# A gated delta rule and a ternary layer on one core: where the chain of states starts, how the first inverses are grouped, and the order of the last units

## The chip, the cores and the metric

The kernel runs on one core of one Trainium2 chip. The metric is the time of one execution on the device in microseconds; the profile gives the span of one profiled execution, from its first to its last instruction.

## The reference, cut to what matters

The input x has 4 sequences of 4096 tokens of 512 numbers; there are 16 heads of 32. All is fp32.

```python
def _L0_attn_ref(x, Wv, Wo, Wg, Wb):          # x is layer-normalised already
    rk = x.reshape(Bb, Tt, H, dd)
    rk = rk / max(norm(rk, axis=-1), 1e-12)   # keys
    wk = rk shifted by one token              # write keys
    v = (x @ Wv.T).reshape(Bb, Tt, H, dd)
    gate = sigmoid(x @ Wg.T)
    beta = sigmoid(x @ Wb.T)
    def step(S, inp):
        pred = einsum('bhk,bhkd->bhd', wk_t, S)
        err = (v_t - pred) * b_t[..., None]
        S = S + wk_t[..., None] * err[..., None, :]
        o = einsum('bhk,bhkd->bhd', rk_t, S) * g_t[..., None]
        return (S, o)
    ...
    return out @ Wo.T
def _L0_ffn_ref(x, weight, ln_gamma, ln_beta):
    xn = layernorm(x) * ln_gamma + ln_beta
    beta = mean(abs(weight))
    w_q = clip(round(weight / (beta + EPS)), -1, 1)
    gamma = max(abs(xn))                       # over the whole tensor
    xq = clip(xn * QB / gamma, -QB + EPS, QB - EPS)
    return (xq @ w_q) * (gamma * beta / QB)
x = x + layernorm(attn(layernorm(x)))
x = x + layernorm(ffn(layernorm(x)))
```

The state S of a head is carried through all 4096 tokens, so the recurrence is serial. The number gamma is a maximum over all tokens, so it is known only behind the last one.

## The kernel before, in words

**Units.** A unit is 32 tokens of each of the 4 sequences, which fills 128 partitions; there are NU = 128 units. Within a unit the recurrence is solved in blocks: a 32 x 32 triangular matrix per head and sequence is built from the products of the keys, inverted, and applied to values and keys; only the state is then carried from unit to unit.

**Blocks of unit k** (they need no state). `load` (L149), `x_stats` (L155, VectorE), `x_norm` (L158, GpSimd), `keys` (L167: ACT makes the tile h, which is stored to DRAM at L171), `keys_turn` (L173: TensorE transposes, ACT copies hT and hN, GpSimd puts a column of the next unit into hN at L189), `key_squares`, `key_sums` (L204), `key_norms` (GpSimd, the power at L213), `values` and `values_rest` (TensorE L233 and L265), `values_out` (VectorE L253), `writes` (the mask times beta, L280), `gates`, `grams` (TensorE L298), `blocks` (ACT L309), `masked` (L317; stored to DRAM). The two mask products run on VectorE for the units of the first group and on GpSimd for all others (`masks`, L270).

**Inverses.** Units are taken in groups, `sizes = [4, 4, 6, 6]` and then 8 each, the last group being 4. `gather` (L325) brings the group's matrices from DRAM so that one partition holds whole matrices, and `invert` (L334) inverts them on VectorE in place: for s from 1 to 30 one product (L343) and one add (L349), each depending on the one before. A group of any size has 60 such instructions; their length grows with the size. The work of a group is spread evenly over a span of steps, between the step in which its units' blocks are there and the step three before its first unit is due in the chain.

**Chain of unit i.** `fetch`, `fetch_inverse`, `expand` (ACT L408), `apply` (TensorE L420), `errors` (TensorE L437 and L444; VectorE makes e at L450 and o at L455), `outputs` (GpSimd L459), `grow` (TensorE L470; VectorE adds into the state, four instructions of L476). Then, one to five units later: `out_turn`, `project` (TensorE L511), `residual` (VectorE L520), `x1_stats`, `x1_norm`, `x1_turn`, `largest` (VectorE L559 fills gmax), `ternary` (TensorE L570) and `finish` (VectorE L582, four stores at L586). `x1_stats`, `project` and `ternary` each use ACT for a sum of squares (L497) and GpSimd for its power (L94).

**Order.** The order of work on every engine is written out by hand. A step is either a plan step (unit i of the chain and unit k of the blocks, list `plan`, L667) or a lead step (blocks of unit k alone, list `lead`, L682). There are `START = sizes[0] + 6` = 10 lead steps, 0 to 9; then plan steps for i = -3, -2, -1 (the chain is only prepared); then from i = 0 every plan step is followed by a lead step until the blocks are 21 units ahead. So the chain's unit 0 is in step 13, eight pairs (a plan step and a lead step) follow, then plain plan steps; behind the blocks' last unit the plan steps hold chain work only. Numbers such as 0.3 in the lists are the places where a share of the inverse work is put. `in_order` (L724) ties each engine to the order in which the instructions are written. All stores and loads are issued by SP, in that same order. One-time work on the weights stands in front and, as `between` (L756), behind the steps 0, 1 and 2.

**Behind the chain.** gamma is made by a maximum on VectorE and a reduction over the partitions on GpSimd (`partition_all_reduce`, L795). The layer's output was computed without the clip; a list of the units whose largest xn reaches the clip is then made (L805 to L834: `ps_gm`, `place`, `hit`, `todo`), and a loop (L840) computes these units anew from xn and x1 in DRAM. With these inputs it runs for one unit.

Of the kernel before, what the change touches and what calls it, by code (L numbers as in the profile page):

```python
# [8 lines left out]
F32 = mybir.dt.float32  # L9
# [4 lines left out]
P = 128  # L14
# [8 lines left out]
def kernel(  # L23
# [85 lines left out]
    with ExitStack() as ph1:  # L109
# [27 lines left out]
        sizes = [4, 4, 6, 6]  # L137
# [29 lines left out]
        def keys(i):  # L167
            my = cx[i]
            my["h"] = wk.tile([P, D], F32, tag="h", name=f"h_{i}")
            nc.scalar.activation(my["h"], my.pop("x"), AF.Identity, bias=my["nb"], scale=my["rs"])  # L170
            nc.sync.dma_start(out=h_d[i], in_=my["h"])  # L171
# [98 lines left out]
        def masks(i):  # L270
            return nc.vector if i < sizes[0] else nc.gpsimd
# [307 lines left out]
        def finish(i):  # L579
# [4 lines left out]
            )  # L584
            for b in range(B):
                nc.sync.dma_start(out=out[b, i * DH : (i + 1) * DH, :], in_=y[quarters(b), :])  # L586
# [50 lines left out]
        def ternary_scale():  # L637
            nc.vector.tensor_reduce(part, wq, AX.X, ALU.add, apply_absolute_value=True)
            nc.vector.tensor_reduce(bsum, part, AX.X, ALU.add)
            ones = wk.tile([P, D], F32, tag="junk", name="ones", bufs=1)  # L640
            nc.gpsimd.memset(ones[:, :P], 1.0 / (D * D))
# [40 lines left out]
        lead = (  # L682
# [6 lines left out]


        FAR = 4 * NP + 5
        START = sizes[0] + 6
# [3 lines left out]
        for i in range(-3, NU + 6):  # L696
            k += 1
            steps.append((i, k))
            if i >= 0 and k < i + FAR:
                k += 1  # L700
                steps.append((None, k))
# [41 lines left out]
        for f in (x_stats, x_norm, keys, keys_turn, key_squares):  # L743
            do(f, 0)
        for f in (x_stats, x_norm, keys):
            do(f, 1)
        do(load, 4)
        do(key_sums, 0), do(key_norms, 0)
        turn_weight("wv", wvbT)
        do(keys_turn, 1), do(key_squares, 1)  # L750
        turn_small("wb", wvbT[:, :, D : D + H])
        turn_small("wg", wvbT[:, :, D + H :])
        do(x_stats, 2), do(x_norm, 2)
        for t_ in tbds:
            nc.vector.memset(t_, 0.0)
        between = {  # L756
            0: (ternary_scale,), 1: (lambda: turn_weight("wo", woT, wm), ternary_round),
            2: (lambda: centred(woT, wm), ternary_centre),
# [3 lines left out]
        for n, (i, k) in enumerate(steps):  # L762
# [5 lines left out]
            for item in lead if i is None else plan:  # L768
# [12 lines left out]

        for n in range(2):
# [4 lines left out]
    with ExitStack() as ph2:  # L787
        once = ph2.enter_context(tc.tile_pool(name="once2", bufs=1))
        wk = ph2.enter_context(tc.tile_pool(name="wk2", bufs=1))
        TOP = QB - EPS  # L790

        gpart = once.tile([P, 1], F32, name="gpart")
        nc.vector.tensor_reduce(gpart, gmax, AX.X, ALU.max)
        gamma = once.tile([P, 1], F32, name="gamma")
        nc.gpsimd.partition_all_reduce(gamma, gpart, P, bass_isa.ReduceOp.max)  # L795
        qs = once.tile([P, 1], F32, name="qs")
        nc.vector.reciprocal(qs, gamma)
        nc.vector.tensor_scalar_mul(qs, qs, QB)
        ys = once.tile([P, 1], F32, name="ys")
        nc.vector.tensor_scalar(ys, gamma, beta, 1.0 / QB, ALU.mult, ALU.mult)  # L800
        ys2 = once.tile([P, 1], F32, name="ys2")
        nc.vector.tensor_tensor(ys2, ys, ys, ALU.mult)


        num = once.tile([P, NU], mybir.dt.int32, name="num")  # L805
        nc.gpsimd.iota(num, pattern=[[1, NU]], base=0, channel_multiplier=0)
        col = once.tile([P, NU], F32, name="col")
        nc.vector.tensor_copy(col, num)
        nc.gpsimd.iota(num[:, 0:1], pattern=[[1, 1]], base=0, channel_multiplier=1)
        row = once.tile([P, 1], F32, name="row")  # L810
        nc.vector.tensor_copy(row, num[:, 0:1])
        ahead = once.tile([P, NU], F32, name="ahead")
        nc.vector.tensor_scalar(ahead, col, row, None, ALU.is_gt)
        ps = bank("ps_gm")
        nc.tensor.transpose(ps[:, :P], gmax, ident)
        umax = once.tile([P, 1], F32, name="umax")
        nc.vector.tensor_reduce(umax, ps[:, :P], AX.X, ALU.max)
        again_ = once.tile([P, 1], F32, name="again")
        nc.vector.tensor_scalar(again_, umax, qs, TOP, ALU.mult, ALU.is_le)
        nc.vector.tensor_scalar(again_, again_, -1.0, 1.0, ALU.mult, ALU.add)  # L820
        ps = bank("ps_place")
        nc.tensor.matmul(ps[:, 0:1], lhsT=ahead, rhs=again_, start=True, stop=True)
        place = once.tile([P, 1], F32, name="place")
        nc.vector.tensor_copy(place, ps[:, 0:1])
        hit = once.tile([P, NU + 1], F32, name="hit")
        nc.vector.tensor_scalar(hit[:, :NU], col, place, again_, ALU.is_equal, ALU.mult)
        both = once.tile([P, 2], F32, name="both")
        nc.vector.tensor_copy(both[:, 0:1], row)
        nc.vector.memset(both[:, 1:2], 1.0)
        ps = bank("ps_list")  # L830
        nc.tensor.matmul(ps[0:1, :NU], lhsT=both[:, 0:1], rhs=hit[:, :NU], start=True, stop=True)
        nc.tensor.matmul(ps[0:1, NU : NU + 1], lhsT=both[:, 1:2], rhs=again_, start=True, stop=True)
# [61 lines left out]
```

## Time and profile before

| | us |
|---|---|
| median of 3 runs | 2456.01 (2452.75 to 2457.76) |
| the profiled execution | 2456.91 |
| its span | 2454.2 |
| TensorE busy | 2336.5 |
| VectorE busy | 1907.9 |
| ScalarE (ACT) busy | 1680.2 |
| GpSimd (POOL) busy | 1684.3 |

How to read the profile's rows: a digit string shows the busy share of each fortieth of the span (61 us), in tenths. A row of a timeline gives start and length in us, engine, line, operation, output and inputs, and, in brackets, for how long the engine was idle before and what ended it. PE is TensorE, PEld its weight loads, DVE is VectorE, SPq the queue of SP. In a table of stretches each engine has its busy time and its number of instructions, then the clock that TensorE was granted, the busy share of the DMA engines and what they moved. In the chain that ended last, "issue" is time in which the engine waited for nothing that the profile shows.

### The profile page before, as it was taken

The numbers are of one execution on the slowest core, as the hardware profiler recorded it, in microseconds if no ns is written. First come the engines' busy times: TensorE is split into PE (matmuls) and PEld (weight loads), VectorE is DVE, ScalarE is ACT, GpSimd is POOL, SyncE is SP. The second block draws the span as 40 slices with busy tenths as digits, with TensorE's granted clock in tenths as the row PEclk, the third lists the DMA queues.
The fourth block names the chain that finished last, engine by engine and source line by source line (L and its number), as shares of the span: only waits on it lengthen the run. The fifth ranks groups of instructions, "written<-read, shape, count | busy, mean of one in ns | idle before, by whom it ended". The sixth has DMA issues, their size and how long they took to land.

```text
span 2454.2 us, 69871 instructions
## 1 busy us (share of the span) xinstructions
PE 2336.5 (95%) x26657; PEld 1554.0 (63%) x26657; DVE 1907.9 (78%) x2928; ACT 1680.2 (68%) x3484; POOL 1684.3 (69%) x2702
## 2 busy tenths in 40 slices
PE   5778999999999999999999999999999999999995
PEld 4556666666666666666666666666666666555552
DVE  5888777988788888888788887878888787887642
ACT  5556667776777777677777767777776777665652
POOL 5988877877777776767777677777767776422221
PEclk8889999999999999999999999999999999999997
DMA  5576666767676766676676767667676766746442
GB/s 152 142 188 167 196 172 191 197 198 200 203 202 192 205 183 202 178 208 183 193 198 177 215 179 206 184 195 195 173 218 177 208 184 184 191 140 169 141 120 64
DMA packets 765372, 445.93 MB, mean 182 GB/s; under 512 B 591056, under 2 KB 591056, under 8 KB 765040
## 3 DMA queue, kind: packets, MB, share of 16 engines
q1 hardware_dynamic: 765040, 441.48, 64.4%
q8 instruction: 212, 3.47, 0.6%
q14 instruction: 120, 0.98, 0.1%
HBM read 205.07 MB, written 235.14 MB: 179 GB/s over the span
## 4 chain that ended last, share of the span: by engine, by line
PE 83%; POOL 6%; DVE 4%; ACT 2%; issue 2%; DMA 1%; SPq 1%; DVEq 0%; POOLq 0%; ACTq 0%
PE ps_wo L511 19%; PE ps_y L570 16%; PE ps_v L233 9%; PE ps_v L265 7%; PE ps_ds L470 6%; PE ps_u L420 5%; PE ps_gram L298 5%; PE ps_f L444 5%; PE ps_w L420 4%; PE ps_f L437 3%; PE ps_oT L491 2%; POOL rn L213 2%; PE ps_xn L491 2%; PE ps_hT L179 2%; DVE na L349 1%
## 5 line engine op out<-in xcount | busy, mean ns | idle before, releaser
L511 PE MATMUL ps_wo<-woT,oT 128*128 128x512 f32 x1024 | 473.7, 605 | 1.6 <-ACT oT L504 1.6
L570 PE MATMUL ps_y<-wq,xn 128*128 128x512 f32 x1024 | 462.2, 594 | 0.0
L343 DVE TENSOR_TENSOR pr<-na 128x336 f32<-128x336 f32 (+25 forms) x540 | 437.1, 809 | 12.4 <-DMA x<-in_L_attn_x_dram 0.6
L349 DVE TENSOR_TENSOR na<-na,pr 128x336 f32<-128x336 f32 (+25 forms) x540 | 431.5, 799 | 12.2
L213 POOL TENSOR_TENSOR rn<-ss,mhalf 128x16 f32<-128x16 f32 x128 | 379.3, 2964 | 10.7
L476 DVE TENSOR_TENSOR state<-ps_ds,state 32x512 f32<-32x512 f32 x508 | 347.9, 685 | 20.3 <-PE ps_ds L470 14.9
L309 ACT COPY nat<-ps_gram 32x512 f32<-32x512 f32 x512 | 294.7, 576 | 33.8 <-PE ps_gram L298 29.4
L408 ACT COPY tbd<-q 32x512 f32<-32x512 f32 x512 | 313.1, 612 | 7.0
L532 POOL TENSOR_SCALAR vpe_c<-acc_c 128x1 f32<-128x1 f32 x128 | 24.3, 190 | 422.5 <-ACT junk_c L497 422.5
L511 PEld LDWEIGHTS ps_wo<-woT,oT 128*128 128x128 f32 x1024 | 184.0, 189 | 200.9 <-issue 183.7
L233 PE MATMUL ps_v<-wvbT,hN 128*128 128x288 f32 x1024 | 281.6, 419 | 26.6 <-POOL hN L189 26.6
L570 PEld LDWEIGHTS ps_y<-wq,xn 128*128 128x128 f32 x1024 | 185.2, 191 | 185.2 <-issue 184.5
L552 ACT ACTIVATE xn<-ps_xn,lnb,lng 128x128 f32<-128x128 f32 x512 | 192.2, 457 | 100.2 <-PE ps_xn L491 100.2
L253 DVE TENSOR_TENSOR v<-ps_v,nrm 128x256 f32<-128x256 f32 x256 | 107.3, 420 | 182.2 <-issue 140.9
L497 ACT ACTIVATE junk_y<-ps_y 128x512 f32<-128x512 f32 x128 | 76.5, 597 | 250.1 <-PE ps_y L570 250.1
L265 PE MATMUL ps_v<-wvbT,hN 128*128 128x256 f32 x1024 | 247.3, 385 | 0.3 <-DVE v L253 0.3
L233 PEld LDWEIGHTS ps_v<-wvbT,hN 128*128 128x128 f32 x1024 | 189.5, 195 | 73.6 <-POOL hN L189 29.3
L420 PE MATMUL ps_u<-tbd,v 128*32 128x128 f32 x4096 | 209.0, 276 | 0.0
L420 PE MATMUL ps_w<-tbd,h 128*32 128x128 f32 x4096 | 205.7, 273 | 0.1
L265 PEld LDWEIGHTS ps_v<-wvbT,hN 128*128 128x128 f32 x1024 | 188.2, 194 | 22.4 <-issue 1.0
L520 DVE SCALAR_TENSOR_TENSOR x<-ps_wo,rstd_b,xr 128x512 f32<-128x512 f32 x128 | 96.1, 751 | 113.5 <-POOL rstd_b L94 100.7
L450 DVE TENSOR_TENSOR e<-ps_f,bet 128x512 f32<-128x512 f32 x127 | 87.7, 690 | 116.8 <-PE ps_f L444 116.8
(146 smaller groups left out, 4373.7 us busy)
## 6 DMA issues: line engine op xcount, KB each, us to landing
x<-in_L_attn_x_dram SPq DMA_DIRECT2D x512, 64.0 KB
h_d<-h SPq DMA_DIRECT2D x128, 256.0 KB
v_d<-v SPq DMA_DIRECT2D x128, 256.0 KB
nat_d<-nat SPq DMA_DIRECT2D x128, 256.0 KB
na<-nat_d SPq DMA_DIRECT2D x256, 128.0 KB
q_d<-na SPq DMA_DIRECT2D x64, 512.0 KB
q<-q_d SPq DMA_DIRECT2D x256, 128.0 KB
h<-h_d SPq DMA_DIRECT2D x128, 256.0 KB
```

The costliest lines, as they stand in the source:

```text
L213: nc.gpsimd.tensor_tensor(rn, ss, mhalf, ALU.pow)
L233: nc.tensor.matmul(ps[:, : half + 2 * H], lhsT=my["hN"][:, k, :], rhs=wvbT[:, k, half:], start=(k == 0), stop=(k == KC - 1),)
L265: nc.tensor.matmul(ps[:, :half], lhsT=my["hN"][:, k, :], rhs=wvbT[:, k, :half], start=(k == 0), stop=(k == KC - 1),)
L309: nc.scalar.copy(nat[s].rearrange("p (j q) t -> p j q t", j=HQ), ps[s].rearrange("p j (q t) -> p j q t", q=NQ)[:, :, :, s],)
L343: nc.vector.tensor_tensor(prs[s], bcast(na[:, :, s, s + 1 :], [P, np_, s, m], 2), bcast(na[:, :, :s, s], [P, np_, s, m], 3), ALU.mult,)
L349: nc.vector.tensor_tensor(na[:, :, :s, s + 1 :], na[:, :, :s, s + 1 :], prs.pop(s), ALU.add)
L408: nc.scalar.copy(tbds[i % NBD][s, :, s], q[s])
L420: nc.tensor.matmul(ps[quarters(j), qq * P : (qq + 1) * P], lhsT=src[:, hd * DH : (hd + 1) * DH], rhs=tbd[:, j * NQ + qq, :], start=True, s ...
L476: nc.vector.tensor_tensor(S[s, :, :, s], psd[s].rearrange("p b (q d) -> p b q d", q=NQ)[:, :, :, s], S[s, :, :, s], ALU.add,)
L511: nc.tensor.matmul(ps, lhsT=oT[:, k, :], rhs=woT[:, k, :], start=(k == 0), stop=(k == KC - 1))
L552: nc.scalar.activation(xn[:, k * P : (k + 1) * P], ps[:, k * P : (k + 1) * P], AF.Identity, bias=lnb[:, k : k + 1], scale=lng[:, k : k + 1],)
L570: nc.tensor.matmul(ps, lhsT=xn[:, k * P : (k + 1) * P], rhs=wq[:, k, :], start=(k == 0), stop=(k == KC - 1),)
```

## The change

- The groups of inverses are 2, 2, 2, 2, 4, 4 units, then 8 each (the last one has 8, too). `START` is 6: six lead steps, then i = -3, -2, -1, then unit 0 of the chain in step 9. Pairs go on until the blocks are 21 units ahead again, so there are twelve of them. Groups 0 to 6 have the steps 4-5, 6-7, 8-10, 11-14, 15-18, 19-26 and 27-33 (before, groups 0 to 4 had 6-9, 10-14, 16-22, 23-31 and 32-37).
- The lead steps in front have a list of their own, in which loads, statistics, keys and squares are one unit further ahead and the turn of the keys comes early; the lead steps of the pairs keep the old list, now named `beside`. The order in front is changed to fit, and the weight work is spread behind the steps 0 to 3.
- The stores of h for units 0, 1 and 2 are issued by ACT's queue; so are the output stores of units 125 to 127 and half of the output stores of the loop.
- Plan steps end with i = 126. The rest of the last units is written out in an order of its own. In it, the reduction of gamma over the partitions is made by TensorE transposes and VectorE, and the list of units is made before `ternary(127)` and the last three `finish`.
- The tiles behind the chain are cut from the pools in use; no new pool is opened.

```diff
-        sizes = [4, 4, 6, 6]
+        sizes = [2, 2, 2, 2, 4, 4]
...
-            nc.sync.dma_start(out=h_d[i], in_=my["h"])
+            (nc.scalar if i < 3 else nc.sync).dma_start(out=h_d[i], in_=my["h"])
...
-            return nc.vector if i < sizes[0] else nc.gpsimd
+            return nc.vector if i < 4 else nc.gpsimd
...
+            queue = nc.scalar if i > NU - 4 else nc.sync
             for b in range(B):
-                nc.sync.dma_start(out=out[b, i * DH : (i + 1) * DH, :], in_=y[quarters(b), :])
+                queue.dma_start(out=out[b, i * DH : (i + 1) * DH, :], in_=y[quarters(b), :])
...
-        lead = (
+        beside = (
...
+        lead = (
+            (AHEAD, 6, load), (AHEAD, 4, x_stats), (AHEAD, 4, x_norm), (AHEAD, 2, keys_turn),
+            (AHEAD, 1, key_sums), (AHEAD, 1, key_norms), (AHEAD, -1, blocks), (AHEAD, 0, values),
+            (AHEAD, 2, key_squares), (AHEAD, 3, keys), (AHEAD, -1, masked), 0.3,
+            (AHEAD, 0, values_out, half), (AHEAD, 0, values_rest), (AHEAD, 0, writes), 0.35,
+            (AHEAD, 0, values_out, 0), (AHEAD, -1, gates), (AHEAD, 0, grams), 0.35,
+        )
...
-        START = sizes[0] + 6
+        START = 6
...
-        for i in range(-3, NU + 6):
+        for i in range(-3, NU - 1):
...
-        for f in (x_stats, x_norm, keys, keys_turn, key_squares):
-            do(f, 0)
-        for f in (x_stats, x_norm, keys):
-            do(f, 1)
-        do(load, 4)
-        do(key_sums, 0), do(key_norms, 0)
+        for f, i in (
+            (x_stats, 0), (x_norm, 0), (keys, 0), (keys_turn, 0), (load, 4),
+            (x_stats, 1), (x_norm, 1), (keys, 1), (load, 5), (key_squares, 0),
+            (x_stats, 2), (x_norm, 2), (key_sums, 0), (key_norms, 0), (keys_turn, 1),
+        ):
+            do(f, i)
...
-            0: (ternary_scale,), 1: (lambda: turn_weight("wo", woT, wm), ternary_round),
-            2: (lambda: centred(woT, wm), ternary_centre),
+            0: (ternary_sums,), 1: (ternary_scale, lambda: turn_weight("wo", woT, wm)),
+            2: (ternary_round, lambda: centred(woT, wm)), 3: (ternary_centre,),
...
-            for item in lead if i is None else plan:
+            for item in plan if i is not None else lead if n < START else beside:
...
+        N = NU - 1
+        for f, i in (
+            (again, N), (errors, N), (out_turn, N - 1), (x1_turn, N - 3), (outputs, N),
+            (x1_stats, N - 2), (finish, N - 5), (x1_norm, N - 2), (largest, N - 3),
+            (project, N - 1), (out_turn, N), (x1_turn, N - 2), (project, N), (residual, N - 1),
+            (x1_stats, N - 1), (x1_norm, N - 1), (largest, N - 2), (residual, N),
+            (ternary, N - 4), (finish, N - 4), (x1_stats, N), (x1_norm, N), (x1_turn, N - 1),
+            (ternary, N - 3), (largest, N - 1), (x1_turn, N), (largest, N), (finish, N - 3),
+            (ternary, N - 2),
+        ):
+            do(f, i)
...
-        nc.gpsimd.partition_all_reduce(gamma, gpart, P, bass_isa.ReduceOp.max)
...
+        nc.vector.tensor_reduce(umax, ps[:, :P], AX.X, ALU.max)
+        nc.tensor.transpose(ps[0:1, P : 2 * P], umax, ident)
+        gamma, gall = some(1), some(P)
+        nc.vector.tensor_reduce(gall[0:1, 0:1], ps[0:1, P : 2 * P], AX.X, ALU.max)
+        nc.vector.tensor_copy(gall[0:1, 1:], gall[0:1, 0:1].to_broadcast([1, P - 1]))
+        nc.tensor.transpose(ps[:, 2 * P : 2 * P + 1], gall[0:1, :], ident[0:1, 0:1])
+        nc.vector.tensor_copy(gamma, ps[:, 2 * P : 2 * P + 1])
...
+        do(ternary, N - 1)
...
+        do(ternary, N)
+        for i in range(N - 2, NU):
+            do(finish, i)
...
-                nc.sync.dma_start(out=out[b, bass.ds(u * DH, DH), :], in_=y[quarters(b), :])
+                (nc.sync if b % 2 == 0 else nc.scalar).dma_start(
+                    out=out[b, bass.ds(u * DH, DH), :], in_=y[quarters(b), :]
+                )
```

## The prediction

> **What bounds the kernel now.** The page comes first, for the share of each engine over the span.
>
> ```profile
> PE   5778999999999999999999999999999999999995
> DVE  5888777988788888888788887878888787887642
> POOL 5988877877777776767777677777767776422221
> PEclk8889999999999999999999999999999999999997
> ```
>
> TensorE is full except in the first four slices and the last one. Between them nothing that the change touches can gain. So the question has two parts: the head (up to about 420 us) and the tail (from the last unit of the chain). In the timeline of VectorE every unit of the chain is marked by its one `e` (L450). I write e(i) for its start: e(0) at 150.18, e(8) at 344.23, e(12) at 420.65, e(126) at 2378.38 us. From e(12) to e(105) they lie 17.89 us apart. Second view: busy time in stretches cut at these marks.
>
> ```profile
> core 0: us, PE busy (x) PEld busy (x) DVE busy (x) ACT busy (x) POOL busy (x), PEclk, DMA share, GB/s
> 86.30:97.90 11.60, 9.39 (x64) 7.36 (x63) 11.22 (x20) 5.45 (x12) 10.80 (x15) 0.83 0.66 172
> 150.18:173.29 23.11, 17.14 (x242) 13.24 (x241) 20.76 (x43) 14.92 (x27) 17.98 (x29) 0.98 0.62 164
> 218.67:244.94 26.27, 22.17 (x252) 15.75 (x252) 21.98 (x34) 17.76 (x36) 21.50 (x34) 0.94 0.65 172
> 244.94:268.65 23.71, 23.17 (x258) 16.11 (x259) 19.73 (x40) 15.29 (x32) 21.61 (x35) 1.00 0.68 206
> 383.42:401.31 17.89, 17.89 (x209) 11.97 (x210) 12.65 (x25) 13.02 (x28) 11.87 (x21) 1.00 0.53 171
> 2250.00:2300.00 50.00, 47.14 (x612) 28.57 (x611) 35.30 (x57) 29.74 (x66) 13.97 (x29) 1.00 0.53 148
> ```
>
> The first row is a lead step (blocks only): VectorE is busy 97% of it and GpSimd 93%; TensorE, though listed as busy, runs at a clock of 0.83. The next three are pairs (a chain step and a lead step), at 23 to 26 us; then a plain step. The last row holds 3.7 chain-only steps of 13.53 us, so a chain unit is 12.75 us of TensorE. A block unit is then 17.89 - 12.75 = 5.1, and a pair needs 23.0 of TensorE.
>
> Third, the timeline of VectorE and GpSimd in a lead step, for the price of the inverses.
>
> ```profile
> 84.14 1.68 DVE L343 TENSOR_TENSOR pr<-na 128x396 f32<-128x396 f32 x1
> 85.86 0.57 DVE L349 TENSOR_TENSOR na<-na,pr 128x396 f32<-128x396 f32 x1
> 84.13 1.26 POOL L317 TENSOR_TENSOR nat<-nat,mb 128x512 f32<-128x512 f32 x1
> 122.64 0.22 DVE L343 TENSOR_TENSOR pr<-na 128x60 f32<-128x60 f32 x1
> 145.46 0.66 DVE L343 TENSOR_TENSOR pr<-na 128x480 f32<-128x480 f32 x1
> ```
>
> Start to start, 60 elements take 0.26 us and 480 take 0.70: 0.197 us fixed and 1.05 ns an element. Every group, whatever its size, is 60 such instructions in one dependent row, with 9,920 elements for each pair of units: 11.8 + 10.4 us for 2 units = 22.2; 4 units 32.6, 6 units 43.0, 8 units 53.4.
>
> Fourth, the chain that ended last, in the tail.
>
> ```profile
> 2417.54 0.30 DVE gpart L793
> 2417.84 3.95 issue
> 2421.78 0.38 POOL gamma L795
> 2422.23 6.62 issue
> 2429.11 0.60 POOL rstd_y L94
> ```
>
> From 2417.8 to 2429.1 everything stands behind one GpSimd reduction, listed as 0.38 us, with 4.0 us before it and 6.6 behind it in which GpSimd shows no work.
>
> **The head, part by part.** *First keys stored by ACT's queue.* Now the store of h(0) is issued by SP at 14.39, though h(0) is ready at 7.7, because SP first has loads of x and of three weights in its row. The tile of h(2) is that of h(0), so its write waits:
>
> ```profile
> 21.68 0.81 ACT L170 ACTIVATE h<-x,nb_a,rstd_a 128x512 f32<-128x512 f32 x1 [4.76 <-DMA x<-in_L_attn_x_dram]
> ```
>
> The Trainium skill speaks against this edit (DMA: Bandwidth & Descriptors, "Issuing engines are not separate DMA queues": queues of different engines share the same 16 DMA engines, so only issue time is saved). By the rule the store would still share the DMA with 2 MB of weights and the gain would be near zero; by the row it is issue order that counts, 14.39 against about 7.8, and up to 4.8 us are free. What follows limits it: the first ps_v runs from 17.89 to 21.4, so the first v comes at 21.8 instead of 24.17. I take 2.4 us, with 0 and 2.4 as bounds. ACT pays 3 issues of about 0.4 us (the SP rows' price), in time in which it waits.
>
> *Steps 0 to 3.* From v(0) to v(4) VectorE now needs 42.4 us (24.17 to 66.58). Of these, ACT waits 4.5 for ps_beta and 4.6 for wm, and GpSimd waits 20.3 us in six places for mv_a. The new lead order (statistics and keys one unit earlier, the turn of keys first, the weight work over four steps) can remove the two ACT waits and some of the rest: I take 31 us, 7.8 a step, near the 7.2 to 7.7 between GpSimd's rn (L213) at steps 4 and 5 now, where no weight work stands. Bounds 27 and 42. The first inverse then starts at 21.8 + 31 + 1 = 54 (48 to 66) instead of 75.4.
>
> *Steps 4 to 8: groups of 2 units.* Group 0 has steps 4 and 5, group 1 steps 6 and 7, group 2 steps 8 to 10. VectorE also does 2.1 us of block work a step (from starts: st 0.72, aggr 0.10, ss 0.59, v twice 0.34). Sum: 22.2 + 22.2 + 7.4 + 5 x 2.1 + 0.6 (the last mask) = 62.9 us. Now a lead step's share is 32.6/4 + 2.1 = 10.2 and steps take 10.2 to 11; then it is 13.2, so VectorE alone sets the pace. Add the fight for the port: the first row of the third view took 1.68 where its neighbour of the same size took 0.57, while GpSimd's mask ran. The Trainium skill (SBUF — State Buffer, "SBUF: two separate sides") says that a VectorE instruction with two SBUF inputs and a GpSimd one that reads SBUF exclude each other for the whole instruction. By the rule each of the two masks of a step would cost up to 1.1 to 1.3 us, 13 us in five steps; group 0 now shows seven hits in four steps, 7.4 us in all. I take 7 (0 to 13), and 2 for small waits. e(0) = 54 + 62.9 + 7 + 2 = 126 (111 to 140), 24 us earlier than now, where four steps at the present pace (44 us) would have been expected.
>
> *Twelve pairs instead of eight.* VectorE's fixed part of a pair is 2 x 2.1 + 5.9 (state 2.79, y, x1, gmax, e, o about 0.63 each) = 10.1. With the groups' shares: pair 0: 24.9; 1 and 2: 21.2; 3 and 4 (4 units in 4 steps): 26.4; 5 to 8: 18.2; 9 to 11 (8 units in 7 steps): 25.4. The larger of this and TensorE's 23.0, added up, is 24.9 + 46 + 52.8 + 92 + 76.2 = 291.9. The same sum for the present eight is 23.1 + 161 = 184.1, measured 194.05, so 1.24 more for each. For twelve: 291.9 + 14.9 = 307 (292 without it; 320 if the dense six take 29 as the pair at 218.67 would with 4.4 us more VectorE work). e(12) = 126 + 307 = 433. At e(12) both kernels have the same 33 block steps behind them, and the same plan ahead. Now it is at 420.65, and this already holds the step from pairs to plain ones (21.3 instead of 17.9); the changed kernel still has that ahead: +3.4. Head: 433 + 3.4 - 420.65 = +15.8 us (between -15 and +35).
>
> **The chain-only stretch.** VectorE then does 5.9 + 53.4/8 = 12.6 a step while a group of 8 runs. Now that is so from e(107) to e(113), and these steps take 14.05 on average; with the last group of only 4 they take 13.53. The changed kernel's last group has 8, over ten such steps: 4 more x 0.52 = +2. The rest of the plan is unchanged.
>
> **The tail.** Order of TensorE behind the last ps_f (2391.8): oT and xn, wo(126) until 2396.6, oT(127), wo(127) until 2401.2 (now 2405.7, since y(123) goes ahead of it), y(123), xn(126), y(124), xn(127), y(125). From wo(127) to gmax(127) the rows give about 11.5 us, with two waits on ACT: gmax is complete at 2412.7 (now 2417.5), y(125) ends then, too. Now comes the replacement of the reduction: three transposes and their copies at 0.75 + 0.2 us a hop (the hop of ps_place and place now: 2431.28 to 2432.03), gamma at 2415.7, qs and again_ at 2416.5; y(126) sits ahead of ps_place and ends at 2419; place, hit and list as now give todo at 2421.3 instead of 2434.1. So 11.3 us of stall become 3 of hops and 2.5 of y(126). Then some is given back: the stores of y(125) wait on ACT behind the squares of y(127) (2425.3); y(127) takes the same tile, so waits until they land (about 2429), and ys, ys2 and the loop's first xq stand behind it on VectorE: xq at 2430.1 instead of 2439.15. From there to the end the rows give 15.05; one unit in the loop, its 6.3 us of ps_again at a clock of 0.62[...], and 1 us less as two queues store. End 2444: -10.5 (-15 to -6; lower if ps_again keeps its clock, 2.9 us).
>
> The remaining edits (masks by number, ones by VectorE, iota earlier, tiles from the old pool) cost below 1 us each beside waits of several us, and nothing is late behind them.
>
> **Sum.** 15.8 + 2 - 10.5 = +7 us by the middle values; the largest part, the twelve pairs, I set 2 us lower (305), since light pairs may take up what dense ones leave. So +5 against a profiled execution of 2456.9 (span 2454.2 and 2.7 around it). The median shown is 2456.0: 2461.
>
> **Rivals.** *Main case, 0.48:* as summed, own range 2453 to 2470. VectorE's saturation in steps 4 to 8 and in six pairs returns what the early chain brings; the tail pays most of it back. *The early chain holds, 0.27:* lead steps keep 10.7 us, pairs keep 24.3: e(0) at 108 to 116, e(12) at 400 to 408, head -10 to -15, with the tail 2431 to 2440. For it: VectorE is busy only 80% from 80 to 400 us, and pairs at 280 to 300 us have holes. Against: 13.2 us of instructions don't fit in 10.7. This is the case on the other side; it decides when the dense pairs stay below 25.5 us and e(0) comes before 117. *GpSimd as bound, 0.20:* at 21.5 busy and 34 gaps of 0.08 a pair, it is 92% full already, and a denser VectorE stretches it (10.8 us a lead step against 7.2 without inverses): dense pairs at 30, 2472 to 2482. *The lead order doesn't help, 0.05:* steps 0 to 3 keep 42 us, so e(0) at 137: 2472.
>
> **The numbers.** About 0.2% (4.9 us) is what a measurement of this kernel tells from no change: bounds 2451.1 and 2460.9. Of the main case I put 0.22 within, 0.23 above and 0.03 below. The early-chain case is faster by 0.25 and 0.02 within; the two others are slower. Faster 0.28, same 0.24, slower 0.48. The range from 2435 to 2478 leaves out the outer part of both rivals.
>
> **What would show it.** e(0) near 126; lead steps 4 to 7 at 13 to 14 us with VectorE at 95%; pairs 3, 4, 9, 10 and 11 at 27 to 28, the others below 25; e(12) at 428 to 438; ten chain-only steps near 14.05; the hole on TensorE behind gmax gone, todo near 2421 plus the shift of the head. It is wrong if dense pairs take 24 us, or if the first inverse starts before 48 us.

## The result, and the profile after

The changed kernel takes 2482.7 us (median of 4 runs, 2478.91 to 2483.43) against 2456.84 beside it: a ratio of 1.0105 (95% interval 1.0088 to 1.0123). It is slower by 26 us where +5 was forecast, and lies outside the range. Its profiled span is 2481.3 us against 2454.2: +27.1.

The page of the changed kernel, busy shares of the slices (62 us each here):

```profile
PE   6578998999999999999999999999999999999997
...
DVE  4889868887878788887888888888888888788442
...
POOL 5568878777777777777777777777677777522221
PEclk8789999999999999999999999999999999999998
```

TensorE now has 6 5 7 8 in the first four slices, where it had 5 7 7 8, and an 8 in the seventh where it had a 9. The place of the loss is read from the marks e(i), the starts of VectorE's `e`:

| mark | before | after | after minus before |
|---|---|---|---|
| first instruction of an inverse | 75.41 | 70.86 | -4.6 |
| e(0) | 150.18 | 136.81 | -13.4 |
| e(9) | 365.54 | 366.14 | +0.6 |
| e(12) | 420.65 | 452.16 | +31.5 |
| e(18) to e(106) | | | +34.1 |
| e(126) | 2378.38 | 2414.63 | +36.25 |
| end of the span | 2454.2 | 2481.3 | +27.1 |

The chain does start 13 us earlier. It loses 45 us in the twelve pairs, keeps the lag for 90 steps, and gets 9 us back in the tail. Stretches of the changed kernel, with the columns of the same view before:

```profile
core 0: us, PE busy (x) PEld busy (x) DVE busy (x) ACT busy (x) POOL busy (x), PEclk, DMA share, GB/s
80.00:100.00 20.00, 10.48 (x59) 7.73 (x60) 18.83 (x45) 7.90 (x14) 11.82 (x18) 0.76 0.40 92
207.95:236.30 28.35, 23.61 (x257) 16.27 (x255) 27.00 (x51) 18.39 (x38) 22.98 (x35) 0.90 0.81 185
335.03:366.14 31.11, 26.70 (x261) 17.72 (x261) 17.99 (x37) 17.62 (x37) 20.64 (x38) 0.89 0.57 158
366.14:395.62 29.48, 26.23 (x272) 18.02 (x272) 25.88 (x41) 19.05 (x40) 24.08 (x33) 1.00 0.79 187
543.30:561.19 17.89, 17.89 (x209) 11.97 (x209) 13.71 (x20) 13.01 (x28) 14.21 (x25) 1.00 0.77 180
2290.00:2340.00 50.00, 46.69 (x562) 28.03 (x555) 25.86 (x42) 31.38 (x67) 12.69 (x30) 1.00 0.68 176
```

First a stretch of lead steps: VectorE is 94% busy, as forecast, and TensorE's clock is down to 0.76. Then three pairs. The one at 207.95 has VectorE at 95%. The one at 335.03 takes 31.1 us although *no* engine is near full: VectorE 18.0, GpSimd 20.6, TensorE 26.7 at a clock of 0.89. The forecast put this pair at 23.0 plus 1.24. The last two rows, a plain step and the chain-only stretch, have the old pace.

In front, ScalarE (ACT) waited twice for the weight work before the change (timeline of ACT; the brackets give the idle time before):

```profile
29.49 0.16 ACT L644 COPY beta<-ps_beta 128x1 f32<-128x1 f32 x1 [4.46 <-PE ps_beta L643]
...
48.84 2.56 ACT L630 ACTIVATE woT<-woT,wm 128x512 f32<-128x512 f32 x4 [4.59 <-DVE wm L628]
```

It still does so twice in the changed kernel, and it still stands once, for 5.89 us, in the first 25 us (4.76 before, in a row that the prediction shows):

```profile
22.87 0.35 ACTq L172 DMA_DIRECT2D h_d<-h  x1
23.27 0.58 ACT L184 COPY hT<-ps_hT 128x512 f32<-128x512 f32 x1 [5.89 <-DMA x<-in_L_attn_x_dram]
...
52.29 2.56 ACT L632 ACTIVATE woT<-woT,wm 128x512 f32<-128x512 f32 x4 [5.25 <-DVE wm L630]
...
64.49 2.56 ACT L632 ACTIVATE wq<-wq,part 128x512 f32<-128x512 f32 x4 [5.04 <-DVE part L630]
```

The copy hT reads no x. The row above it, of ACT's own queue, shows whose wait it is: the third store of h, ready since 17.4, is issued only at 22.87, once an earlier load of x has landed that shares its semaphore, and the copy stands behind it.

And the tail, where the reduction of gamma stood (timeline of VectorE):

```profile
2450.16 0.29 DVE L832 TENSOR_REDUCE many<-ps_gm 128x1 f32<-128x128 f32 x1
...
2451.65 0.16 DVE L838 COPY many<-ps_gm 128x1 f32<-128x1 f32 x1 [0.31 <-PE ps_gm L837]
...
2455.39 0.16 DVE L848 COPY many<-ps_place 128x1 f32<-128x1 f32 x1 [2.76 <-PE ps_place L847]
...
2456.43 0.28 DVE L854 CAST todo<-ps_list 1x129 int32<-1x129 f32 x1 [0.50 <-PE ps_list L852]
```

The maximum over the partitions is there 1.65 us after the first reduction starts; the list of units (`todo`) is complete at 2456.7. Less the lag of 36.25 at e(126) that is 2420.5; 2421.3 was forecast.

### The profile page after: what moved, and what is told of

It is laid out like the page before. It is cut to its first block, busy times and chain, and to the rows that moved or that the text cites. A ratio compares the mean times of both kernels' runs of the same rounds, so it can differ in the third digit from the quotient of the medians.

```text
span 2481.3 us, 70012 instructions
## 1 busy us (share of the span) xinstructions
PE 2350.8 (95%) x26659; PEld 1563.0 (63%) x26659; DVE 1934.2 (78%) x3053; ACT 1680.3 (68%) x3485; POOL 1676.9 (68%) x2700
## 4 chain that ended last, share of the span: by engine, by line
PE 78%; DVE 9%; POOL 3%; DMA 3%; SPq 3%; issue 2%; ACT 1%; ACTq 0%; DVEq 0%; POOLq 0%
PE ps_wo L512 18%; PE ps_y L571 15%; PE ps_v L234 8%; PE ps_v L266 7%; PE ps_ds L471 5%; PE ps_u L421 4%; PE ps_gram L299 4%; PE ps_f L445 4%; PE ps_w L421 4%; DVE pr L344 3%; DVE na L350 3%; PE ps_f L438 3%; PE ps_oT L492 2%; PE ps_xn L492 2%; PE ps_hT L180 2%
## 5 line engine op out<-in xcount | busy, mean ns | idle before, releaser
L344 DVE TENSOR_TENSOR pr<-na 128x120 f32<-128x120 f32 (+8 forms) x600 | 450.1, 750 | 14.0 <-issue 0.3
L350 DVE TENSOR_TENSOR na<-na,pr 128x120 f32<-128x120 f32 (+8 forms) x600 | 444.3, 740 | 14.4
L214 POOL TENSOR_TENSOR rn<-ss,mhalf 128x16 f32<-128x16 f32 x128 | 377.9, 2953 | 10.6
L310 ACT COPY nat<-ps_gram 32x512 f32<-32x512 f32 x512 | 294.8, 576 | 31.5 <-PE ps_gram L299 27.0
L234 PE MATMUL ps_v<-wvbT,hN 128*128 128x288 f32 x1024 | 288.0, 427 | 28.7 <-POOL hN L190 27.9
```

The costliest lines, as they stand in the source:

```text
L214: nc.gpsimd.tensor_tensor(rn, ss, mhalf, ALU.pow)
L234: nc.tensor.matmul(ps[:, : half + 2 * H], lhsT=my["hN"][:, k, :], rhs=wvbT[:, k, half:], start=(k == 0), stop=(k == KC - 1),)
L310: nc.scalar.copy(nat[s].rearrange("p (j q) t -> p j q t", j=HQ), ps[s].rearrange("p j (q t) -> p j q t", q=NQ)[:, :, :, s],)
L344: nc.vector.tensor_tensor(prs[s], bcast(na[:, :, s, s + 1 :], [P, np_, s, m], 2), bcast(na[:, :, :s, s], [P, np_, s, m], 3), ALU.mult,)
L350: nc.vector.tensor_tensor(na[:, :, :s, s + 1 :], na[:, :, :s, s + 1 :], prs.pop(s), ALU.add)
```

## The experiments

Three suspects came out of the traces: the new groups, the new front, and something in the long middle. All kernels below were timed against the kernel before on the same chip; a ratio stands with its interval.

**1. The parts alone.** The first kernel keeps only the tail and the output queues:

```diff
-        sizes = [2, 2, 2, 2, 4, 4]
+        sizes = [4, 4, 6, 6]
-        START = 6
+        START = 10
-        (nc.scalar if i < 3 else nc.sync).dma_start(out=h_d[i], in_=my["h"])
+        nc.sync.dma_start(out=h_d[i], in_=my["h"])
```

`lead`, the order in front and `between` are as before the change, too.

> The new order of the last units and the output queues, with the head as before: groups of 4, 4, 6, 6, ten lead steps, the old front order, list and queue. If the loss lies in the head alone, as the marks e(i) of the two traces say (lag +34.1 us at e(13), +36.3 at e(126), end 9.2 us nearer to e(126)), this is faster than the kernel before by 9 to 10 us: 2446 to 2448. The rival, that the tail's gain needs the other head or is given back, would give 2452 or more.

Measured: 2464.52, 1.0027 (1.0018 to 1.0036). The expectation was refuted, and by the run from which least was asked: its plan is that of before up to e(126), and still it is 19.3 us late there. It loses 7.7 us by e(12), and then whole steps stall: e(19) comes 22.25 us after e(18), and e(35) 24.1 after e(34), where 17.4 to 17.9 is the pace. ACT waits for a load there (waits of ACT around e(19)):

```profile
engine line waited for: us in total, times, longest us
...
ACT tbd L409 <- DMA q<-q_d: 4.1, 3, 3.0
```

> The changed kernel with the groups of 4, 4, 6, 6 and ten lead steps put back; front order, lead list, queue and tail stay new. Theory: small groups and the early chain are what cost most (VectorE without slack in steps 4 to 8 and in six pairs), so this recovers 25 to 32 us: 2451 to 2458, with e(0) near 150 to 155 and e(12) near 420 to 427. Rival (the new front order costs most): recovers 5 to 10 us only, 2473 to 2478.

This kernel has the old `sizes` and `START = 10`, with the new front. Measured: 2470.78, 1.0055 (1.0032 to 1.0077), with four such stalls of 2.7 to 6.9 us; +25.8 at e(126). That is neither the 2451 to 2458 of the theory nor the 2473 to 2478 of its rival.

> The changed kernel with the old front: old start order, old lead list, weight work behind steps 0 to 2, keys stored by SP; small groups, six lead steps and tail stay new. Theory: the new front doesn't make steps 0 to 3 faster (first inverse at 70.9 us where 54 had been forecast), so this is equal or 2 to 6 us faster: 2477 to 2483, first inverse at 64 to 70. Rival (the new front gains as it was meant to, and something else is late): slower by 5 us or more.

This one keeps the small groups, with the old front. Measured: 2477.5, 1.0089 (1.0075 to 1.0104); e(0) at 133.47 and e(12) at 445.55. So the new front is no help: without it the chain starts 3.3 us *earlier*.

```diff
-            2: (ternary_round, lambda: centred(woT, wm)), 3: (ternary_centre,),
+            2: (lambda: sums_scaled(wm), ternary_round),
+            3: (lambda: centred(woT, wm), ternary_centre), 4: (lambda: centred(wq, part),),
```

> The changed kernel with ACT's part of the weight centring put one step behind VectorE's part, so that ACT doesn't stand 5.3 and 5.0 us for the sums in steps 2 and 3. Theory: these two waits hold up hT, the grams and so the masks of the next step; without them the first inverse starts at 60 to 63 instead of 70.9 and, VectorE setting the pace from there, e(0) and all that follows come 7 to 10 us earlier: 2473 to 2476. Rival (steps 0 to 3 are held by the DMA or by GpSimd's waits for the statistics): less than 3 us gained.

Here ACT's half of the weight work comes one step behind VectorE's half. Measured: 2478.37, 1.0085 (1.0071 to 1.01); e(0) at 132.4, so the two ACT waits of the front are worth 4.4 us there, less than the 7 to 10 that were expected.

**2. Why does even the tail alone lose in the middle?** The busy share of the DMA queue between 600 and 1800 us gives a trace of it. In front the kernel before, then the changed one (packets, MB, share of 16 engines):

```profile
q1 hardware_dynamic: 399641, 230.59, 68.8%
```

```profile
q1 hardware_dynamic: 399087, 230.19, 75.6%
```

Packets and bytes are the same within 0.2%, but a packet takes 36.4 ns instead of 33.0 (share x 1200 us x 16 / packets). The first guess was the second queue.

```diff
-            queue = nc.scalar if i > NU - 4 else nc.sync
+            queue = nc.sync
```

> The tail alone, as in the run with only the new tail, but every DMA issued by SP: no DMA on ACT's queue anywhere. That run had the head and the plan as before, and yet lost 7.7 us by e(12) and 4.4 and 6.2 us in two steps near e(19) and e(35), where ACT waited for the load of q; its DMA packets took 75.7% of the DMA engines' time from 600 to 1800 us where the kernel before has 68.8% for the same bytes. Theory A: the second DMA queue in the program is what makes every packet take longer; without it the share is 69% again, no step is late, and the tail's gain stands: 2446 to 2449. Theory B (placement of tiles, or the new code behind the chain, moves the DMA): share stays near 75%, time stays at 2460 to 2468.

> The kernel before with one edit: the output stores of units 125, 126 and 127 (12 DMAs at the very end) are issued by ACT. Theory A: the mere presence of the second queue raises the share of the DMA engines from 600 to 1800 us from 68.8% to about 75%, 600 us and more before its first DMA, and the kernel is slower by 5 to 15 us with a wider spread: 2461 to 2472. Theory B: no change, 2454 to 2458, share 69%.

> The changed kernel with every DMA issued by SP (first keys, last units, loop). Theory A: the DMA share falls to 69%; what of the head's 34 us came from slower loads is recovered, 5 to 15 us: 2466 to 2478. The rest is VectorE's saturation: e(12) not before 435. Theory B or the head being VectorE's alone: 2479 to 2484; the stall of h(2) behind the weights comes back for 2 us.

The tail kernel without any DMA on ACT: 2463.95, 1.0037 (1.0022 to 1.0051), share 77.1%. The kernel before with the stores of three units on ACT: 2453.45, 0.9992 (0.9984 to 1.0), share 68.6%. The changed kernel with all DMAs on SP: 2485.0, 1.0115 (1.01 to 1.0129), share 76.3%. The second queue is not the cause, in any of the three. (The last of them says something of the front, too: its first v comes at 28.63 us, against 26.01 in the changed kernel.)

What all slow kernels share is smaller: `todo`, of 129 numbers (516 B, placed as 544), is now cut from the pool `once`, which lies ahead of the working pools, so that each of their tiles starts 544 B later. The large tiles that started at multiples of 256 B (x at 68352, na at 76544) now start at multiples of 32 only. (The small tiles of the pool `stat` started at multiples of 32 to 256 before, too; "aligned" below means the large ones.) Two kernels put this right, two put it wrong in the kernel before:

```diff
-        todo = once.tile([1, NU + 1], mybir.dt.int32, name="todo")
+        todo = once.tile([1, 256], mybir.dt.int32, name="todo")[:, : NU + 1]
```
```diff
         rbeta = once.tile([P, 1], F32, name="rbeta")
+        spare = once.tile([P, 8], F32, name="spare")
+        nc.vector.memset(spare[:, 0:1], 0.0)
```

> The changed kernel with todo's tile padded from 129 to 256 numbers (1024 B), so that every tile of the pools behind it starts at a multiple of 256 B again as it did before the change; nothing else differs. Theory C (the moved tiles make every DMA packet about a tenth longer, and late loads stretch the pairs and stall single steps): DMA share of the middle stretch back at about 69% from 75.6%, 10 to 20 us recovered, 2462 to 2474, e(12) near 433 to 440 instead of 452. Rival (the share comes from the order of issues, the placement is nothing): share stays at 75 to 76%, 2479 to 2484.

> The kernel of tail and queues only (old groups, old front, new last units) with the same padding. Theory C: 2446 to 2449, which is what the tail alone was expected to give, share 69%, no jumps of the chain at steps 19 and 35. Rival: 2462 to 2466, share 75 to 76%.

> The kernel before the change with an unused tile of 32 B ahead of the working pools, so that all their tiles move by 32 B; one tiny memset is added and nothing else. Theory C: share of the middle stretch rises from 68.8% to about 75%, slower by 5 to 15 us (2461 to 2471). Rival: no change, 2454 to 2459, share 69%.

> The same with an unused tile of 64 B. Theory C leaves two cases open: if a start at a multiple of 64 B is enough, share 69% and 2454 to 2459; if 128 or 256 B is needed, share about 75% and 2461 to 2471. Rival: no change.

Measured: the tail kernel with aligned tiles 2445.35, 0.9953 (0.994 to 0.9966), no stalls; the kernel before moved by 32 B 2473.06, 1.0072 (1.0056 to 1.0089); moved by 64 B 2465.75, 1.0041 (1.0022 to 1.006), share 76.0%. The same view of the aligned tail kernel, then of the kernel before moved by 32 B:

```profile
q1 hardware_dynamic: 399607, 231.00, 68.4%
```

```profile
q1 hardware_dynamic: 403171, 230.00, 77.2%
```

So the placement is shown from both sides: 32 unused bytes cost the kernel before 17 us, and the right start gives the tail kernel 19 us back. But the changed kernel itself, aligned, stays at 2480.01, 1.0098 (1.0084 to 1.0112): its share falls to 67.9% and its e(12) only to 447.2. The theory holds for the packets and explains about 3 of its 26 us.

**3. Groups and front at aligned tiles.** Two more kernels, the second and third of above with the padded tile, complete a square.

> Aligned tiles, new front and tail, but the old groups of 4, 4, 6 and 6 and the chain behind ten lead steps. Theory D: like the kernel of the aligned tail, 2445 to 2451 (the misaligned one took 2470.8, with single stalls that should be gone). Rival (front costs for itself): 2455 or more.

> Aligned tiles, old front, but the small groups and the chain behind six lead steps. Theory D: the small groups keep their whole cost of about 30 us against the aligned tail, 2470 to 2478. Rival (the small groups suffered only from the placement): 2445 to 2455.

| us (ratio, interval) | groups 4, 4, 6, 6; chain behind ten | groups 2, 2, 2, 2, 4, 4; behind six |
|---|---|---|
| old front | 2445.35 (0.9953, 0.994 to 0.9966) | 2472.32 (1.0073, 1.0059 to 1.0086) |
| new front | 2450.66 (0.9981, 0.9972 to 0.999) | 2480.01 (1.0098, 1.0084 to 1.0112) |

The small groups with the early chain cost 27 and 29 us, the new front 5 and 8. So the loss adds up: -10.6 for the tail (2445.35 against 2455.94), +27.0, +7.7 and about 2.7 for the moved tiles give +26.8, and 25.9 was measured. With the tiles moved, the four were 2464.52, 2477.5, 2470.78 and 2482.7: the placement costs 19 to 20 us with the old groups and 3 to 5 with the new ones.

**4. What holds the pairs?** The forecast used TensorE and VectorE alone. In the first trial the dependent products and sums of the groups 0 to 6 are not made (tiles still moved):

```diff
-            for s in range(1, DH - 1):
+            for s in range(1, DH - 1) if firsts[g] >= 24 else ():
```

> The changed kernel without the 60 products and adds of each of the groups 0 to 6 (units 0 to 23); their inverses are then the identity plus the masked products. Theory (VectorE sets the pace in steps 4 to 8 and in the dense pairs): steps 4 to 8 fall from 13.8 to 8 to 9 us, e(0) at 110 to 117, all twelve pairs at 23 to 25 us, e(12) at 395 to 410. Rival (GpSimd or the DMA bounds the pairs): pairs 3, 4, 9, 10 and 11 stay above 27 us.

Measured: 2459.0, 1.0009 (1.0003 to 1.0016). e(0) comes at 109.97, so the inverses' work on VectorE does set the pace of the lead steps; but the twelve pairs take 314 us, as with the inverses in. With aligned tiles the same trial is cleaner:

> The changed kernel with aligned tiles (as in the run with the padded tile) and with the work of the inverses of units 0 to 23 left out: the 60 products and sums of each of the first seven groups, so the inverse there is the identity with the masked products. Theory D (small groups cost VectorE more, and that sets the pace of the lead steps and of the pairs): e(0) near 110, the twelve pairs fall from 311 to 275 to 290 us, e(12) at 385 to 400, 2420 to 2435. Rival E (the pairs are set by something else than VectorE's inverses, such as GpSimd or the order of issues): pairs stay near 310, e(12) near 420, 2450 to 2459.

Measured: 2448.88, 0.9971 (0.9961 to 0.9982); pairs 300.6 us, between the two theories; e(12), at 412.2, and the time are close to rival E. Its busy times in three pairs:

```profile
core 0: us, PE busy (x) PEld busy (x) DVE busy (x) ACT busy (x) POOL busy (x), PEclk, DMA share, GB/s
331.05:355.19 24.14, 23.58 (x261) 16.22 (x262) 10.86 (x20) 17.68 (x37) 18.89 (x35) 1.00 0.73 186
355.19:388.48 33.29, 26.41 (x261) 17.89 (x262) 10.58 (x19) 17.64 (x37) 18.95 (x35) 0.90 0.64 207
388.48:412.19 23.71, 23.37 (x261) 16.30 (x262) 10.58 (x20) 17.68 (x37) 18.88 (x35) 1.00 0.74 190
```

VectorE is busy for 10.6 us in all of them. Yet one takes 33.3 us and its neighbours 24. The wait in the long one:

```profile
engine line waited for: us in total, times, longest us
DVE v L254 <- DMA v_d<-v: 12.1, 1, 12.1
```

VectorE may not write the next v until an older v has been stored. That sends the reader to SP, which issues the stores. In the changed kernel's pair at 335.03 (timeline of SP, start and length; then of VectorE):

```profile
336.26 0.65 SPq L244 DMA_DIRECT2D gr<-gb  x1
338.86 0.56 SPq L245 DMA_DIRECT2D gr<-gb  x1
339.52 0.39 SPq L320 DMA_DIRECT2D nat_d<-nat  x1
340.00 1.77 SPq L588 DMA_DIRECT2D out_dram<-y  x4
341.87 0.37 SPq L524 DMA_DIRECT2D x_d<-x  x1
342.28 0.46 SPq L260 DMA_DIRECT2D v_d<-v  x1
```

```profile
322.17 0.42 DVE L254 TENSOR_TENSOR v<-ps_v,nrm 128x256 f32<-128x256 f32 x1
...
345.38 0.42 DVE L254 TENSOR_TENSOR v<-ps_v,nrm 128x256 f32<-128x256 f32 x1 [9.07 <-DMA v_d<-v]
```

SP has hardly any free time: over this pair it spends 21.5 us in some 40 issues and 9.6 in gaps, and most of the gaps are waits for a DMA to land (waits of SP over the pair):

```profile
SPq L245 <- DMA gr<-gb: 6.2, 3, 2.4
SPq L172 <- ACT nat L310: 1.5, 1, 1.5
SPq L331 <- DMA nat_d<-nat: 1.2, 1, 1.2
```

The largest share has one source. The second `gr` copy writes rows that the first writes too, so it waits until that one has landed, here from 336.91 to 338.86. All later stores stand behind. The v that was complete at 322.6 is stored at 342.28, 19.7 us late (the k-th store in SP's row is that of the k-th v), and as there are two tiles for v, VectorE stands until 345.38. So the last two runs take one `gr` copy of the units 6 to 39 away, its issue and its wait together, and nothing else, with and without the inverses' work (the gates of these units are then not shifted by a row):

```diff
+            if 6 <= i < 40:
+                nc.sync.dma_start(out=gr, in_=gb[:, 1, :])
+            else:
                 nc.sync.dma_start(out=gr[1:, :], in_=gb[: P - 1, 1, :])
                 nc.sync.dma_start(
                     out=gr[::DH, :], in_=first[(0 if i == 0 else DH - 1) :: DH, :]
                 )
```

> The aligned kernel without inverse work for units 0 to 23, and with the shifted gates of units 6 to 39 fetched by one copy of the tile instead of two (so these gates are not shifted by a row): SP loses one issue of 0.56 us and one wait of 1.9 to 2.2 us per unit, about 5.4 us a pair, and nothing is added anywhere. Theory F (in the pairs SP's queue is full, 19 to 25 us of issues and 5 to 9 us of waits, and holds up the stores that VectorE waits for): the long pairs of 28 to 33 us shrink, the twelve pairs fall from 300 to 280 to 288 us, e(12) at 391 to 400 instead of 412, about 15 us faster than its parent. Rival (SP only looks full because what it waits for is late): pairs stay at 296 to 302.

> The changed kernel with aligned tiles and the same single copy for the gates of units 6 to 39, with all inverse work in it. Theory F and VectorE together: twelve pairs from 311 to 295 to 303 us, e(12) at 431 to 439, 2465 to 2472. If VectorE's load alone holds the pairs: 308 to 312, 2476 to 2481. If SP alone: pairs near 285 to 290, 2453 to 2460.

Measured: 2406.02, 0.9798 (0.9781 to 0.9814), and 2472.39, 1.007 (1.0053 to 1.0087). The first gained more than expected, the second just missed what was expected of SP's row and VectorE together. The light one's pairs, three rows of the same view as above:

```profile
306.65:330.36 23.71, 23.37 (x261) 16.30 (x262) 11.06 (x21) 17.67 (x37) 18.88 (x35) 1.00 0.83 236
330.36:354.06 23.70, 23.36 (x261) 16.30 (x261) 10.57 (x19) 17.66 (x37) 18.84 (x35) 1.00 0.75 229
354.06:377.77 23.71, 23.37 (x261) 16.30 (x262) 10.58 (x20) 17.68 (x37) 18.87 (x35) 1.00 0.78 205
```

Each takes 23.7 us, with TensorE busy for 23.4 of them, at full clock. The four kernels, all with aligned tiles:

| twelve pairs, us (median, us) | two gate copies | one gate copy |
|---|---|---|
| inverses of units 0 to 23 in | 311.3 (2480.01) | 304.1 (2472.39) |
| their work left out | 300.6 (2448.88) | 268.7 (2406.02) |

Either relief alone gives 7 or 11 us, both together 42.6. The inverses' work and SP's row are nearly equally full there, and each hides what the other costs. The lag of the v stores says the same (mean over the pairs): 11.3 and 15.6 us with two copies, 4.7 and 5.5 with one. In the kernel before it is 12.1 already: SP's row was behind before the change, but only for eight pairs. What is left with one copy and the inverses in:

```profile
309.03:332.74 23.71, 23.36 (x261) 16.30 (x262) 17.66 (x31) 17.71 (x37) 20.64 (x35) 1.00 0.76 200
332.74:356.45 23.71, 23.36 (x261) 16.30 (x262) 17.36 (x37) 17.71 (x37) 20.50 (x37) 1.00 0.61 181
356.45:384.78 28.33, 26.23 (x272) 18.02 (x272) 26.17 (x41) 20.85 (x43) 24.12 (x34) 1.00 0.74 206
410.50:440.50 30.00, 26.49 (x260) 18.08 (x260) 23.84 (x34) 17.89 (x36) 25.53 (x35) 0.89 0.61 160
```

The light pairs (the first two rows) are at TensorE's 23.7; the dense ones take 28 and 30, with VectorE busy for 26.2 and 23.8 us and GpSimd for 24.1 and 25.5. Which of these two holds them was not separated by a run. In the first of the two dense pairs VectorE is busy for 92% of the time; in the second the waits name GpSimd (waits of PE, then of SP, from 410.50 to 440.50):

```profile
PE ps_v L234 <- POOL hN L190: 4.1, 1, 4.1
```

```profile
SPq L323 <- POOL bet L280: 8.9, 1, 8.9
```

**5. A version that beats both.** The aligned tail kernel is that: 2445.35 against 2455.94 beside it. Added to it, the split weight work changes nothing:

> A candidate: the aligned tail kernel (old groups, old front, new last units) with ACT's part of the weight work one step behind VectorE's. The waits of ACT that this removes were worth 4.4 us at e(0) in the changed kernel; here e(0) 145 to 150, 2440 to 2446.

Measured: 2445.71, 0.9957 (0.9943 to 0.997), e(0) at 150.48. With the old groups these waits are not on the path. A gate copy that keeps the shift and needs no wait was not tried.

## Why the prediction was wrong, point by point

The sum was +5.3 in the profile's terms and +27.1 came. Two steps failed: the lead steps 0 to 3 were not made shorter (44.85 us from the first v to the first inverse, where 32 had been put), and the twelve pairs took 315.35 us instead of 305, since SP's row and the start of the tiles (7.2 and 4.1 us) stood in no term. By the prediction's own steps:

| step | forecast | measured | adds to the miss |
|---|---|---|---|
| steps 0 to 3: first inverse at | 54 | 70.86 | +16.9 |
| steps 4 to 8: from there to e(0) | 72 | 65.95 | -6.0 |
| twelve pairs | 305 | 315.35 | +10.4 |
| behind e(12) | +3.4 | +2.6 | -0.8 |
| chain-only stretch | +2 | +2.2 | +0.2 |
| tail | -10.5 | -9.1 | +1.4 |

*First keys by ACT's queue: the size was right, the place was not.* The first v comes at 26.01, not 21.8 (24.17 before). But the queue is not to blame. With all DMAs on SP and the rest of the change as it is, the first v comes at 28.63, so ACT's queue is worth 2.6 us there, where 2.4 had been put; at the first inverse 0.8 is left of it (71.68 against 70.86). What cost more than that is the new order of the front around it: with SP issuing all in front, the first v comes at 23.66 in the old order (the third run above) and at 28.63 in the new one. From 15.67 on SP has twelve issues of x in its row, where it had eight, and ACT stands for 5.89 us behind the issue of the third store. The rule of the Trainium skill that I set aside for the row (DMA: Bandwidth & Descriptors, "Issuing engines are not separate DMA queues": only issue time is saved) would have given near zero. That is 2.6 us off at the first v, and within 1 us at the first inverse.

*Steps 0 to 3 at 31 us: the step that failed most.* They take 44.85 us from the first v to the first inverse. "Can remove the two ACT waits" was wrong: the wait for `ps_beta` (4.5 us) went, but that for `wm` stayed (4.6, now 5.25) and one of 5.04 for `part` came, since VectorE makes both in the very step in which ACT uses them. The split kernel takes them away and gains 4.4. "Some of the rest" did not go either: GpSimd's waits for `mv_a` between the first v and the first inverse are four and 17.0 us, and were four and 17.3 (the 20.3 in six places of the prediction count two that end before the first v). At aligned tiles the old front reaches its first inverse at 66.7 and the new one at 70.0: the reordering itself loses 3 us. What holds these steps beyond the ACT waits stays open; without them they still take 40.2 us. The rival that named this, with e(0) at 137, had a chance of 0.05; e(0) came at 136.8.

*Steps 4 to 8: right in mechanism.* VectorE is 94% busy and its inverses set the pace; leaving out the inverses brings e(0) from 136 to 112. The sum without port was 62.9, so port and waits together cost 3.1 us, not 9. By the skill's rule of the shared port (SBUF — State Buffer, "SBUF: two separate sides") up to 13 were to be expected; no run here shows that much, and none separates the port.

*Twelve pairs: the number was near, the model was not.* "The larger of TensorE and VectorE" gave 291.9, the surplus of 1.24 a pair made it 307, and it was set to 305. SP was never counted. Its row adds 7.2 (311.3 less 304.1) and the moved tiles 4.1 (315.35 less 311.3). Split into the five pairs with dense inverses (3, 4, 9, 10 and 11) and the other seven, in us:

| | two engines alone | with 1.24 each | changed | aligned | aligned, one gate copy |
|---|---|---|---|---|---|
| five dense pairs | 129.0 | 135.2 | 143.2 | 144.8 | 140.9 |
| seven others | 162.9 | 171.6 | 172.1 | 166.5 | 163.2 |

So the two engines describe the seven once SP's row is relieved, in their sum (a full light pair takes TensorE 23.7 rather than 23.0, and the pairs 1 and 2 take less). They don't describe the dense ones: these take 2.4 us each more than the sum even then, for a cause that stays open. That 304.1 is near 305 is luck: the surplus, spread over all pairs, covers what the dense ones lack. I took it from the pairs before as a size and didn't ask for its cause; SP's row, late there already, may be a part of it, but no run measured that in the kernel before.

*"Tiles from the old pool ... cost below 1 us": wrong.* Counted by its instructions, the edit costs nothing. It moved every working tile by 544 B, lengthened the average packet by a tenth, and hid in the changed kernel behind the larger losses: about 3 us there, 19 in the kernel with the tail alone.

*Chain-only stretch and tail: right.* In the tail, gamma, the list and the loop's first xq all came within 0.9 us of the forecast, once the head's lag is taken off, and `ps_again` took 6.1 us (6.3). Its granted clock is 0.58 in the trace before, not the prediction's 0.62, and 0.60 in the changed one.

*Rivals.* "The early chain holds" asked for dense pairs below 25.5 us and e(0) before 117; neither came. "GpSimd as bound" gave the right total for a reason that the runs do not bear out: with SP relieved a pair with 20.6 us of GpSimd work goes at 23.7. For dense pairs it stays open, as said, and their mean of 28.6 us is below the 30 that it asked for.

## What to carry to other kernels

Before a stage is made denser, add up every queue in it, the issuing one too: issues times their price, plus the waits that stand in its row; where two are near full, relief of one shows a small part of what there is (7 and 11 us here), and only both together show it (43). A part of a change that "does nothing" is best tested alone: here it carried 19 us of loss that covered a gain of 10. And a tile added to an early pool moves all tiles behind it, so compare the time of a DMA packet before and after.

## What the runs showed of the hardware that was not expected

*The start of a tile.* With the large tiles at multiples of 256 B a packet took 33.0 ns on average; moved by 32, 64 or 544 B it took 36.8, 36.2 and 36.4, and moved by 1024 B, in the two kernels with the padded tile, 32.9 and 33.0. Packets and bytes agree within about 1%. The Trainium skill has a rule that fits in sign (DMA: Bandwidth & Descriptors, "How a descriptor splits into AXI transactions": a transaction must start from a multiple of 256 B, so a descriptor that doesn't start there costs additional beats). No run here shows the transactions themselves, and whether 128 B would do was not tried.

*The price of an issue.* A DMA cost SP mostly 0.37 to 0.65 us each, and up to 0.8 in some rows of four. In pairs of 24 to 31 us that makes 15 to 22 us. The rule cited above calls the time saved by issuing elsewhere usually small; here about 5.4 us of SP's row in a pair, issues and waits of the second gate copy, decided over 31.9 us in the twelve pairs (300.6 less 268.7), where VectorE did not hold them.
